# A deformable convolution and two gated recurrences on one core: forty column places for each parity, the table's writes on two queues, and the last tiles' norms and sums in another order

## The chip, the core and the metric

The kernel runs on one core of a Trainium2 chip. A core has TensorE (PE: matrix products and transposes into PSUM), VectorE (DVE), ScalarE (ACT), GpSimd (POOL) and SyncE (SP); DMA transfers are started by SP, POOL or ACT and carried by 16 DMA engines. The metric is the device time of one execution in microseconds (us), lower is better. All numbers are float32.

## The reference

`x` has 4 images of 256 channels on 64 x 64 positions. Two layers follow one another:

```python
x = x + _L0_conv_ref(_ln_c(x), ...)          # deformable 3x3 convolution of the channel-normalized x
t = _to_tokens(x)                            # (4, 4096, 256)
t = t + _L0_ffn_ref(_ln_t(t), ...)           # gated recurrence over the 4096 positions
x = _from_tokens(t, x)
x = x + _L1_conv_ref(_ln_c(x), ...)          # channel gate
t = _to_tokens(x)
t = t + _L1_ffn_ref(_ln_t(t), ...)
```

The deformable convolution computes 27 numbers per position by an ordinary 3x3 convolution (18 offsets, 9 masks), samples the normalized `x` bilinearly at the nine moved places, multiplies by the masks and applies a 256 x 256 matrix per tap. The recurrence has a projection `x U` and a recurrent product `h V` for each gate; a step is `c = h*c + i*g`, `h = o*tanh(c)`. The channel gate takes mean, maximum and standard deviation over the 4096 positions for each image and channel, subtracts the median of an image's 768 numbers, cubes, weighs and sums them, and multiplies the normalized `x` by a sigmoid of that.

## The kernel before

**Tiling.** A tile is a column of one parity: 128 partitions hold 4 images by 32 rows (even or odd), 256 channels lie along the free axis; 64 columns and two parities give 128 tiles. `RING` is 40 places of one tile each in SBUF (`ring`); a pool "square" has ten buffers of four tiles' size.

**Prepare** (`prepare`, 0 to about 266 us). The 64 columns go in 17 groups, most of four columns. Each group g is loaded from DRAM (`load`), both parities; VectorE takes the statistics (`stats`, `norm_of`; `together` says which groups share one), ScalarE normalizes in place (`norm`); `to_table` writes the normalized columns into a table in DRAM, eight writes a group (four images, two parities), each entry holding two neighbouring columns; PE turns a column (`turned`: four transposes) and multiplies it by the offset weights (`taps`: products into `zacc`); `summed` adds the pieces into `z`, `offsets` turns them into the 27 numbers a position (`om`), `samples` makes of these the places and weights of the sampling, and `keep` stores them in `plan`. The ring is split into two halves of 20 places (`M`), one for each parity, so a group can be loaded only when the table writes of an earlier group have left its place: in iteration g the kernel writes group g+1 and loads group g+4. The writes of both parities and of `plan` are started by SP, the loads from the fifth group on by POOL, in the order in which the loops issue them. `borders` writes zeros around the table (24 writes), on SP, ahead of all other table writes.

**Sampling** (`sample_and_recur`, about 270 to 2240 us). 576 slots; in slot s the kernel issues the gathers of two taps five slots ahead (POOL, indirect, into two "square" buffers), the scaling (ACT), the combination of the four corners (DVE), the transposes (PE, PSUM `tr`), the copy to SBUF (ACT) and 8 products into `acc`. The first gather needs the whole table.

**First recurrence.** Each of the 128 rows of a step is a stretch of 32 rows of an image; 144 steps go over the tiles in `ORDER`, the last 16 tiles first as a warm-up. Step n has its place at slot `step_slot(n)` = 52 + 4.5 n, so about the last 25 steps lie behind the sampling and run alone. A step: `recur` (`ga<-h`, `gb<-h`), `gates_of` (ACT: `tg`, `ti`, `to`, `th`), DVE's `cell` and `h`, and `project_part` for the next step (`ga<-cm`, `gb<-cm`). The gates `i` and `g` share the PSUM bank `ga` (pool of one buffer), `o` has `gb`.

**Fillers.** Everything else around the steps is given to a list (`Spare.give`) with its engine, earliest slot and cost, and `Spare.run` takes from it, in each slot and engine, what fits a budget (`BESIDE` beside the sampling, `ALONE` after it). The fillers: `added` turns `h` back, `add` adds it to the ring and sums the channels; `spread` squares (ACT); `norms` computes 1/std for eight tiles by three Newton steps (DVE, lists `first`, `second`, `last`); `styled` computes for the gate the normalized values and their squares (`y`, ACT, two tiles); `lanes` and `highest` add these up and take the maximum (DVE).

**Tail and gates** (2414 to 2474 us). For the last two pairs `summed` multiplies the sums (`lanes`, `y`) by `own`, a 128 x 4 matrix that adds the 32 partitions of an image, into `ys` (4 x 256); a copy and four transposes bring that to `pq`. `Gate.gates` computes mean, maximum and deviation (`u`), sends them through DRAM to all partitions, ranks them for the median, and computes the gate.

**Second recurrence** (`gated_lstm`, 2480 to 3266 us) and the output follow.

Of the kernel before, what the change touches and what calls it, by code (L numbers as in the profile page):

```python
# [19 lines left out]
P = 128  # L20
# [70 lines left out]
def prepare(tc, pools, const, wts_, x_in, table, errands):  # L91
# [7 lines left out]
    stp, gp, vp, ps_tr, ps_ac, ps_ms, ps_a, ps_b, sm, cm_p, yp = (  # L99
        pools[n] for n in ("chunk", "square", "v", "tr", "acc", "misc", "ga", "gb", "small", "cm", "y")  # L100
    )

    M = RING // 2
    cols = pools["ring"].rearrange("p (e m) c -> p e m c", e=2)
# [107 lines left out]
    def keep(o, w):  # L212
        for e in range(2):
            nc.sync.dma_start(plan[e * (W // OC) + o], w[:, e])
# [22 lines left out]
    def columns(g, lo, hi):  # L237
        return cols[:, :, at[g] + lo : at[g] + hi]

    def load(g, engine):  # L240
        if g < N:
            c, n = groups[g]
            for e in range(2):
                engine.dma_start(columns(g, 0, n)[:, e], x_in[:, e * W + c : e * W + c + n])


    together = [[0]] + [[g, g + 1] for g in range(1, N, 2)]
    sts, norms = {}, {}

    def stats(g):  # L250
        if g >= N:
            return
        gs = next(gs for gs in together if g in gs)
        if g == gs[0]:
            st = sm.tile([P, 20, 6], F32, name="st", tag="sth")
            sts[gs[-1]] = st, []
        st, of = sts[gs[-1]]
        for j in range(groups[g][1]):
            for e in range(2):
                nc.vector.bn_stats(st[:, len(of)], columns(g, j, j + 1)[:, e, 0])  # L260
                of.append((g, j, e))
        if g == gs[-1]:
            rs, low = norm_of(nc, sm, st[:, : len(of)], 1e-6, 20)
            for i, (h, j, e) in enumerate(of):
                norms.setdefault(h, []).append((columns(h, j, j + 1)[:, e, 0], rs, low, i))
# [6 lines left out]
    def to_table(g):  # L272

        c, n = groups[g]
        if c + n == W:
            nc.gpsimd.memset(columns(g, n, n + 1), 0.0)
        if g == 0:
            nc.gpsimd.tensor_copy(again, columns(0, 0, 1)[:, :, 0])
        elif at[g] == 1:
            last = groups[g - 1][1] + more[g - 1]  # L280
            nc.gpsimd.tensor_copy(columns(g, -1, 0), columns(g - 1, last - 1, last))
        if g == N - 1:
            nc.gpsimd.tensor_copy(columns(g, n, n + 1)[:, :, 0], again)
        lo, hi = int(g == 0), n + more[g]
        for e in range(2):
            for i in range(B):
                rows = tabs[i, :, 2 + e : 2 + H : 2].rearrange("x y c -> y x c")
                own = columns(g, lo - 1, hi)[i * R : (i + 1) * R, e]
                both = bass.AP(own.tensor, own.offset, [own.ap[0], [C, hi - lo], [1, 2 * C]])
                nc.sync.dma_start(rows[:, c + lo + 1 : c + hi + 1], both)  # L290
# [3 lines left out]
    def summed(g, zp):  # L294

        b0, b1 = blocks[g]
        z = gp.tile([P, 2, 6, BLOCK], F32, name="z", tag="square")
# [29 lines left out]
    nc.sync.dma_start(columns(0, 0, 2)[:, 0], x_in[:, split - 1 : split + 1])  # L327
    nc.scalar.dma_start(columns(0, 0, 2)[:, 1], x_in[:, W + split - 1 : W + split + 1])
    nc.sync.dma_start(woff, pools["w_off"])
    for g in range(1, 5):  # L330
        load(g, nc.sync)
    nc.sync.dma_start(gr, grid[0])
    nc.sync.dma_start(first, grid[1])
    borders()
# [3 lines left out]
    xt = turned(*(columns(0, 0, 1)[:, e, 0] for e in range(2)))  # L338
# [7 lines left out]
    for g, (c, n) in enumerate(groups):  # L346
# [4 lines left out]
        for j in range(n):  # L351
# [3 lines left out]
            if h < N:  # L355
                xt = turned(*(columns(h, i, i + 1)[:, e, 0] for e in range(2)))
            taps(banks[g], b0, b1 - b0, c + j, now, j == 0, j == n - 1)
            if j == 0 and g:
                summed(g - 1, banks.pop(g - 1))
# [4 lines left out]
        load(g + 4, nc.gpsimd)  # L364
        for o, w in sampled:
            keep(o, w)
        if g > 2 and errands:
            errands.pop(0)(nc)
        sampled = [(o, samples(o, om.pop(o))) for o in [*om] if g > 1 and blocks[g - 1][0] % OC]
        stats(g + 3)  # L370
# [164 lines left out]
class Spare:  # L535
# [6 lines left out]
    def give(self, engine, slot, us, do, room=lambda: True):  # L542
        self.todo.setdefault(engine, []).append((slot, us, do, room))

    def run(self, engine, slot, us, late=6):
        left = self.todo.get(engine, [])
        n = 0
        while n < len(left):
            ready, cost, do, room = left[n]
            if ready <= slot and room() and (cost <= us + 0.3 or slot - ready > late):  # L550
                del left[n]
                us -= cost
                do(slot)
            else:
# [6 lines left out]
def sample_and_recur(  # L561
# [15 lines left out]
    stp, gp, vp, ps_tr, ps_ac, ps_ms, ps_a, ps_b, sm, st, cm_p, yp = (  # L577
        pools[n] for n in ("chunk", "square", "v", "tr", "acc", "misc", "ga", "gb", "small", "state", "cm", "y")
    )
    ring = pools["ring"]  # L580
# [3 lines left out]
    PAIRS = NTILE * K // 2  # L584
    STEPS = len(ORDER)
    AHEAD = 5

# [14 lines left out]
    def gather(n):  # L602

        r = rounds[n] = {"units": [], "sq": [], "w": [], "v": []}
        for i in range(2):
# [5 lines left out]
            sq = gp.tile([P, 4 * C], F32, name="square", tag="square")  # L611
# [84 lines left out]
    def spread(n, k, b, j, slot):  # L696
# [9 lines left out]
        parts = (lo, hi - 2, hi) if b == STEPS // NB + 1 else (lo, hi)  # L706
# [19 lines left out]
    def norms(b, lo, hi, slot):  # L726
# [9 lines left out]
        )  # L736

# [5 lines left out]
        def first(slot):  # L743
# [5 lines left out]
            give("DVE", slot, 0.9, second)  # L749

        def second(slot):
            newton()
            newton()
            give("DVE", slot, 0.4, last)

        def last(slot):
# [6 lines left out]
            if hi > NB:  # L763
                first = max(lo - NB, 0)
                at = slice(ORDER[(b - 2) * NB] + first, ORDER[(b - 2) * NB] + hi - NB)
                nc.vector.tensor_copy(gate.rs[:, at], rs[:, NB + first - lo :])
                nc.vector.tensor_copy(gate.low[:, at], low[:, NB + first - lo :])
                for p in range(first // 2, (hi - NB) // 2):
                    give(
                        "ACT",  # L770
                        slot + 2 + (3 * p if b < STEPS // NB + 1 else 0),
# [5 lines left out]
        give("DVE", slot, 0.9, first)  # L777


    taken = {"xn": 0, "y": 0, "ms": 0, "ys": 0, "cm": 0}  # L780

    def room(tag, n):
        return lambda: taken[tag] < n
# [29 lines left out]
    def styled(b, p, slot):  # L813

        taken["y"] += 1
        n = b * NB + 2 * p
        y = yp.tile([P, 2, 2, C], F32, name="y", tag="y")

        def one(i):
            t = ORDER[n + i]  # L820
            for q, f in enumerate((AF.Identity, AF.Square)):
                normalize(nc, y[:, q, i], place(n + i)[:, 0], gate.rs, gate.low, t, f)

        def other(slot):
            one(1)
            through.update((n, n + 1))
            if n + 4 < STEPS:
                pending.append(y)
                give("DVE", slot + 1, 1.25, lambda s: lanes(y, s))
            else:  # L830
                give("PE", slot + 1, 1.88, lambda s: summed(y, n + 2 == STEPS, s))
                give("DVE", slot + 1, 0.75, lambda s: highest(y))

        one(0)
        give("ACT", slot, 1.15, other)

    def highest(y):
        nc.vector.tensor_max(gate.mx, gate.mx, y[:, 0])
        taken["y"] -= 1

    pending, order = [], []

    def lanes(y, slot):

        nc.vector.tensor_add(gate.lanes, gate.lanes, y)
        pending.pop()
        give("DVE", slot, 0.75, lambda s: highest(y))

    ys = []

    def summed(y, last, slot):

        order.append(last)
        assert not pending and order.index(True) == 1 if last else len(order) == 1
        for x in (gate.lanes, y) if not ys else (y,):
            if not ys:
                ys.append(ps_ms.tile([B, 2, C], F32, name="ys", tag="ys"))
            for i in range(2):
                for q in range(2):
                    nc.tensor.matmul(  # L860
                        ys[0][:, q],
                        gate.own,
                        x[:, q, i],
                        start=(x is gate.lanes and i + q == 0),
                        stop=(last and i + q == 2),
                        skip_group_check=True,
                    )
        if last:
            give("DVE", slot + 1, 0.6, lambda s: nc.vector.tensor_copy(gate.sum, ys[0]))
# [5 lines left out]
    START = 52  # L875
# [14 lines left out]
    def project_part(n, gs):  # L890
        cm = cms[n - n % 2][:, n % 2]
        if gs == SHARED[0]:
# [920 lines left out]
```

## Time and profile before

| what | before |
|---|---|
| runs shown | median 3270.24 us of 10 (3266.06 to 3275.22) |
| profiled execution | 3268.49 us |
| its span and mean granted clock | 3266.7 us, 0.971 |
| busy PE / PEld / DVE / ACT / POOL | 3040.8 / 2819.6 / 2589.9 / 2068.7 / 1580.5 us |
| busy share of PE, DVE, ACT | 93%, 79%, 63% |
| DMA | 829.53 MB, mean 254 GB/s |
| first gather issued on POOL | 269.55 us |
| last `ga<-h` of the first recurrence | 2414.00 us |

All times inside an execution are counted from the span's start. PE stands for matrix products and transposes, PEld for weight loads beside them, SPq for SP's own DMA instructions. A row "A <- B: us, times, longest" says how long an engine stood ahead of writing A because B was not ready. All instructions go through a recording helper, so most rows carry the helper's line (L412) and are told apart by the names of their tiles, out<-in.

### The profile page before, as it was taken

The page shows a single profiled execution, that of the slowest core. Times are in us where ns is not written, and L with a number is a line of the kernel's source. Part 1 is how long each engine was busy: PE and PEld are TensorE (multiplying, and loading weights), DVE is VectorE, ACT ScalarE, POOL GpSimd, SP SyncE. Part 2 cuts the span into 40 slices and gives each one's busy share as a digit, 9 for nine tenths or more (in the row PEclk, how much of TensorE's full clock was granted, in tenths as well). Part 3 has the DMA queues.
Part 4 walks back from the last instruction along what each step waited for, and adds up shares of the span by engine and source line. Part 5 has one row for each costly group of instructions (what it writes and reads, how often), then busy time and mean ns, then how long its engine had stood idle before and what let it go on. Part 6 is the DMA issues. An engine that isn't in the chain of part 4 may idle for free.

```text
span 3266.7 us, 61458 instructions
## 1 busy us (share of the span) xinstructions
PE 3040.8 (93%) x20370; PEld 2819.6 (86%) x20370; DVE 2589.9 (79%) x7218; ACT 2068.7 (63%) x5448; POOL 1580.5 (48%) x1495
## 2 busy tenths in 40 slices
PE   4767889999999999999999999998965999999998
PEld 4666779999999999999999999998854999999997
DVE  3446988888898999999999999995456777777774
ACT  3544566666676776776776776776655666666664
POOL 0005776776676776776677677671000022222221
PEclk8888999999999999999999999999986999999999
DMA  7879999989999999999989989993002244444442
GB/s 235 262 208 325 397 364 329 331 323 344 320 324 344 324 325 345 326 322 342 332 324 338 338 323 330 343 329 103 14 30 81 69 136 145 153 151 151 149 143 86
DMA packets 324278, 829.53 MB, mean 254 GB/s; under 512 B 104640, under 2 KB 112192, under 8 KB 319088
## 3 DMA queue, kind: packets, MB, share of 16 engines
q0 software_dynamic: 181856, 648.64, 55.0%
q1 hardware_dynamic: 141952, 176.61, 16.8%
q8 instruction: 164, 2.69, 0.3%
q14 instruction: 162, 1.33, 0.1%
q10 hardware_dynamic: 144, 0.26, 0.0%
HBM read 702.25 MB, written 123.12 MB: 253 GB/s over the span
## 4 chain that ended last, share of the span: by engine, by line
PE 80%; issue 8%; DMA 5%; DVE 4%; ACT 1%; SPq 1%; POOL 0%; ACTq 0%; POOLq 0%; DVEq 0%
PE acc L412 27%; PE ga L412 12%; PE gacc L412 7%; PE gtr L412 7%; PE tr L412 7%; PE gb L412 6%; DMA square<-table,used 4%; PE ggb L412 4%; PE gga L412 4%; PE zacc L412 2%; PE xt L412 1%; PE om L412 1%; DMA ring<-in_x_dram 1%; DVE st L412 1%; DVE v L412 1%
## 5 line engine op out<-in xcount | busy, mean ns | idle before, releaser
L412 POOL DMA_INDIRECT square<-table,used x1152 | 1380.5, 1198 | 624.2 <-DVE h L412 153.4
L412 DVE SCALAR_TENSOR_TENSOR v<-square,used,v 128x256 f32<-128x256 f32 x3456 | 1411.4, 477 | 56.0 <-ACT v L412 52.4
L412 PE MATMUL acc<-wconv,vt 128*128 128x256 f32 x4608 | 1098.3, 381 | 22.1 <-ACT vt L412 19.1
L412 PEld LDWEIGHTS acc<-wconv,vt 128*128 128x128 f32 x4608 | 832.9, 191 | 122.4 <-ACT vt L412 32.5
L412 ACT COPY vt<-tr 128x512 f32<-128x512 f32 x576 | 335.8, 583 | 520.4 <-PE tr L412 520.2
L412 ACT ACTIVATE v<-square,used 128x256 f32<-128x256 f32 x1152 | 534.9, 512 | 100.8 <-DMA square<-table,used 93.4
L412 PE MATMUL tr<-ident,v 128*128 128x128 f32 x2304 | 348.5, 274 | 17.0 <-DVE v L412 17.0
L412 DVE TENSOR_TENSOR tg<-tg,ti 128x256 f32<-128x256 f32 x284 | 120.2, 423 | 278.9 <-ACT ti L412 278.4
L412 PEld LDWEIGHTS tr<-ident,v 128*128 128x128 f32 x2304 | 273.9, 141 | 32.0 <-DVE v L412 13.3
L412 PEld LDWEIGHTS ga<-cm,Us 128*128 128x128 f32 x2272 | 273.9, 192 | 22.3 <-ACT ti L412 16.3
L412 PE MATMUL ga<-cm,Us 128*128 128x128 f32 x2272 | 279.3, 276 | 11.4 <-ACT ti L412 11.4
L412 PEld LDWEIGHTS ga<-h,Vs 128*128 128x128 f32 x2256 | 272.0, 192 | 5.9
L412 PE MATMUL ga<-h,Vs 128*128 128x128 f32 x2256 | 274.7, 275 | 0.0
L412 POOL DMA_DIRECT2D hd<-sqh x60 | 35.0, 583 | 409.5 <-DVE sqh L412 402.6
L412 POOL DMA_DIRECT2D ring<-hd x240 | 144.9, 632 | 165.3 <-DMA hd<-sqh 145.3
L412 ACT ACTIVATE tg<-gacc,bs 128x128 f32<-128x128 f32 x284 | 88.9, 364 | 185.0 <-PE gacc L412 185.0
L412 DVE TENSOR_TENSOR h<-to,th 128x256 f32<-128x256 f32 x282 | 119.0, 422 | 92.8 <-ACT th L412 92.7
L412 PEld LDWEIGHTS gacc<-h,Vs 128*128 128x128 f32 x1128 | 147.4, 192 | 15.1 <-DVE h L412 7.8
L412 PE MATMUL gacc<-h,Vs 128*128 128x128 f32 x1128 | 150.2, 276 | 6.3 <-DVE h L412 6.3
L412 PEld LDWEIGHTS gb<-cm,Us 128*128 128x128 f32 x1136 | 147.2, 192 | 6.0
L412 PEld LDWEIGHTS gb<-h,Vs 128*128 128x128 f32 x1128 | 146.0, 192 | 5.9
L412 PE MATMUL gtr<-h,Vs 128*128 128x128 f32 x1128 | 149.8, 276 | 0.0
(202 smaller groups left out, 4469.8 us busy)
## 6 DMA issues: line engine op xcount, KB each, us to landing
table<-ring SPq DMA_DIRECT2D x112, 256.0 KB
square<-table,used POOLq DMA_INDIRECT x1152, 6.6
ring<-x2d SPq DMA_DIRECT2D x18, 1024.0 KB
ring<-in_x_dram SPq DMA_DIRECT2D x65, 256.0 KB
x1d<-ring SPq DMA_DIRECT2D x64, 256.0 KB
x2d<-ring SPq DMA_DIRECT2D x16, 1024.0 KB
xd<-sqx SPq DMA_DIRECT2D x64, 256.0 KB
cm<-xd SPq DMA_DIRECT2D x256, 64.0 KB
```

Of the source, the lines that this page charges most:

```text
L412: ins = op(*args, **kw)
```

## The change

1. **Places.** Each parity gets 40 places: the even columns use all of `ring`, the odd ones a new constant tile `squares` of the same shape, which takes the room of the pool "square"; the gathers of sampling use slices of it, still ten in turn. Loads are issued as far ahead as the places allow (`old` names the latest group whose table writes a group's place has to wait for): the first ten groups at the start, partly on POOL, later ones when the writes of `old` lie two groups back.
2. **Queues.** Even table writes go on SP, odd ones on POOL; the writes of `plan` go on POOL; the borders are written after the iteration of the second group.
3. **Statistics** of group g+3 are issued in the middle of the iteration instead of at its end, with groups paired one later; `z` uses another pool.
4. **Steps alone.** Odd steps from the 119th on put `ga` and `gb` into the PSUM banks `acc` and `tr`, which sampling has left; `y` may use freed slices of `squares`; other budgets; in the last block the norms are computed in parts of four and of two tiles, at once and ahead of the list (`urgent`), and written straight into the gate's tiles where they can be.
5. **Sums.** `Gate.add` multiplies 128-column pieces of `lanes` and `y`, as the stationary operand, by `own` into `pq` directly; `ys`, its copy and the four transposes go. For the last two tiles (`ending`) VectorE computes the normalized values and ScalarE the squares, VectorE adds the two tiles.

The diff's core:

```diff
 def prepare(...):
-    M = RING // 2
-    cols = pools["ring"].rearrange("p (e m) c -> p e m c", e=2)
+    M = RING
+    cols = pools["ring"], pools["squares"]
...
     def keep(o, w):
         for e in range(2):
-            nc.sync.dma_start(plan[e * (W // OC) + o], w[:, e])
+            nc.gpsimd.dma_start(plan[e * (W // OC) + o], w[:, e])
...
+    old = []
+    for g, (c, n) in enumerate(groups):
+        own = range(at[g] - 1, at[g] + n + more[g])
+        old.append(max((h for h in range(g - 1) if at[h] + groups[h][1] + more[h] > own[0] and at[h] < own[-1] + 1), default=-1))
...
-    together = [[0]] + [[g, g + 1] for g in range(1, N, 2)]
+    together = [[0], [1]] + [[g, g + 1] for g in range(2, N - 1, 2)] + [[N - 1]]
...
     def to_table(g):
...
-        for e in range(2):
+        for e, engine in enumerate((nc.sync, nc.gpsimd)):
...
-                nc.sync.dma_start(rows[:, c + lo + 1 : c + hi + 1], both)
+                engine.dma_start(rows[:, c + lo + 1 : c + hi + 1], both)
...
-        z = gp.tile([P, 2, 6, BLOCK], F32, name="z", tag="square")
+        z = yp.tile([P, 2, 6, BLOCK], F32, name="z", tag="y")
...
-    for g in range(1, 5):
-        load(g, nc.sync)
+    there = 1
+    while old[there] < 0:
+        load(there, *((nc.sync, nc.sync) if there < 3 else (nc.gpsimd, nc.gpsimd)))
+        there += 1
     nc.sync.dma_start(gr, grid[0])
     nc.sync.dma_start(first, grid[1])
-    borders()
     stats(0)
...
-            if j == 0 and g:
-                summed(g - 1, banks.pop(g - 1))
+            if j == 0:
+                if g:
+                    summed(g - 1, banks.pop(g - 1))
+                stats(g + 3)
...
         if g + 1 < N:
             to_table(g + 1)
-        load(g + 4, nc.gpsimd)
+        while there < N and old[there] <= g - 2:
+            load(there, nc.gpsimd, nc.gpsimd)
+            there += 1
         for o, w in sampled:
             keep(o, w)
+        if g == 1:
+            borders()
...
         sampled = [(o, samples(o, om.pop(o))) for o in [*om] if g > 1 and blocks[g - 1][0] % OC]
-        stats(g + 3)
 class Spare:
     def run(self, engine, slot, us, late=6):
...
                 do(slot)
+                n = 0
 def sample_and_recur(...):
-            sq = gp.tile([P, 4 * C], F32, name="square", tag="square")
+            k = (2 * n + i) % SQUARES
+            sq = squares[:, 4 * k : 4 * k + 4].rearrange("p n c -> p (n c)")
...
-        parts = (lo, hi - 2, hi) if b == STEPS // NB + 1 else (lo, hi)
+        parts = range(lo, hi + 1, {STEPS // NB + 1: 2, STEPS // NB: 4}.get(b, hi - lo))
...
-            give("DVE", slot, 0.9, second)
+            if n0 >= LAST:
+                second(slot)
+            else:
+                give("DVE", slot, 0.9, second)
...
+                if n0 == STEPS - 2:
+                    ending(slot)
+                    return
...
+    def ending(slot):
+        n = STEPS - 2
+        (y, _), (both, _) = result(slot), result(slot)
+        for i in range(2):
+            t = slice(ORDER[n + i], ORDER[n + i] + 1)
+            x = place(n + i)[:, 0]
+            nc.vector.tensor_scalar(y[:, 0, i], x, gate.rs[:, t], gate.low[:, t], ALU.mult, ALU.add)
+            normalize(nc, y[:, 1, i], x, gate.rs, gate.low, t.start, AF.Square)
+        for q in range(2):
+            nc.vector.tensor_add(both[:, q, 0], y[:, q, 0], y[:, q, 1])
+            gate.add(nc, both, (0,), (q,))
+        highest(y, 0)
...
+        other = n % 2 and step_slot(n) > PAIRS + 8
         if gs == SHARED[0]:
-            ga = ps_a.tile([P, 2, NC, P], F32, name="ga", tag="ga")
+            at, tag = (ps_ac, "acc") if other else (ps_a, "ga")
+            ga = at.tile([P, 2, NC, P], F32, name="ga", tag=tag)
...
-            G[n][gs[0]] = ps_b.tile([P, NC, P], F32, name="gb", tag="gb")
+            at, tag = (ps_tr, "tr") if other else (ps_b, "gb")
+            G[n][gs[0]] = at.tile([P, NC, P], F32, name="gb", tag=tag)
...
-    ALONE = {"ACT": (0.3, -1, 1.6, 1.2, 0.3), "DVE": (0.5, -1, 1.3, 1.0, 0.5), "PE": (-1, 0.3, 0.3, 2.0, 0.3)}
+    ALONE = {"ACT": (0.3, -1, 2.9, 0.3, 0.3), "DVE": (0.5, -1, 3.2, 0.8, 0.5), "PE": (-1, 0.3, 0.3, 2.0, 0.3)}
+    END = {"ACT": (0.3, -1, 2.9, 0.3, 0.3), "DVE": (0.4, -1, 4.0, 0.4, 0.4), "PE": (-1, 0.3, 0.3, 2.0, 0.3)}
+    LASTLY = {"ACT": (0.3, -1, 1.0, 0.3, 0.3), "DVE": (0.4, -1, 0.0, 9.0, 9.0), "PE": (-1, 0.3, 9.0, 9.0, 9.0)}
 class Gate:
+    def add(self, nc, x, tiles, sums):
+        new = self.pq is None
+        if new:
+            self.pq = self.pools["misc"].tile([P, 2, NC, B], F32, name="pq", tag="ys")
+        for q in sums:
+            for k in range(NC):
+                for i in tiles:
+                    nc.tensor.matmul(
+                        self.pq[:, q, k],
+                        x[:, q, i, k * P : (k + 1) * P],
+                        self.own,
+                        start=(new and q + k + i == 0),
+                        stop=(len(tiles) == 1 and q + k == 2),
+                        skip_group_check=True,
+                    )
...
-        pq = ps_ms.tile([P, 2, NC, B], F32, name="pq", tag="ys")
-        for q in range(2):
-            for k in range(NC):
-                nc.tensor.transpose(pq[:, q, k], self.sum[:, q, k * P : (k + 1) * P], ident[:B, :B])
+        pq = self.pq
```

## The prediction, written before the changed kernel ran

> **What bounds the kernel now.** I read first the page's forty slices (81.7 us each), to see where the engine that is busy 93% of the span is not:
>
> ```profile
> PE   4767889999999999999999999998965999999998
> PEclk8888999999999999999999999999986999999999
> DMA  7879999989999999999989989993002244444442
> ```
>
> Three places have an idle PE: the first slices, slice 28, and 29 to 30. Between them lies sampling, where PE has 1789.78 of the 1790.00 us from 450 to 2240; only a change of PE's work could help there. The second recurrence (2480 to 3266) has PE busy 97%. The order of the instructions is the same in both kernels from the first sampling slot to the end of sampling and through the second recurrence, so I forecast no change in them and go to the three places.
>
> First the prepare stage, by the table of windows (busy us of PE, PEld, DVE, ACT, POOL; clock; DMA share; GB/s):
>
> ```profile
> 50.00:100.00 50.00, 20.02 (x93) 17.91 (x92) 20.47 (x77) 12.94 (x26) 5.39 (x10) 0.69 0.87 269
> 200.00:250.00 50.00, 32.11 (x162) 29.31 (x163) 20.10 (x78) 20.98 (x44) 3.30 (x6) 0.76 0.60 172
> 300.00:350.00 50.00, 44.96 (x225) 35.64 (x225) 46.65 (x121) 29.95 (x66) 38.18 (x38) 1.00 1.03 407
> ```
>
> No engine is full here, nor are the DMA engines, which reach 1.03 only when the gathers run. So a chain bounds it, and the waits of 0 to 265 us (us in total, times, longest) show its links:
>
> ```profile
> POOL ring L412 <- DMA table<-ring: 88.8, 11, 22.8
> ACT ring L412 <- DVE low L412: 68.8, 8, 15.2
> PEld zacc L412 <- ACT xc L412: 49.9, 8, 13.7
> DVE st L412 <- DMA ring<-in_x_dram: 32.9, 7, 10.0
> ```
>
> Read upwards: the load of a later group waits on POOL until the table writes that still read its place have landed; the statistics wait for the load, the normalization for the statistics, the turning and the taps for that. The order on SP's queue and the end of the stage come from two timelines:
>
> ```profile
> 11.45 22.44 SPq L412 DMA_DIRECT2D table<-zero  x24
> 33.99 11.50 SPq L412 DMA_DIRECT2D table<-ring  x16
> ```
>
> ```profile
> 56.26 0.54 POOL L412 DMA_DIRECT2D ring<-in_x_dram  x1 [22.80 <-DMA table<-ring]
> ...
> 269.55 1.36 POOL L412 DMA_INDIRECT square<-table,used  x1 [58.95 <-DVE fl L412]
> ```
>
> The first table write leaves 22 us late, behind 24 border writes; the first load that has to wait goes at 56.26; the first gather, which needs the whole table, at 269.55 (last table issue 263.4).
>
> Second, the steps of the first recurrence that run alone (PE's timeline):
>
> ```profile
> 2389.21 1.95 PE L412 MATMUL ga<-h,Vs 128*128 128x128 f32 x16
> 2390.99 1.06 PE L412 MATMUL gb<-h,Vs 128*128 128x128 f32 x8
> 2392.39 2.05 PE L412 MATMUL ga<-cm,Us 128*128 128x128 f32 x16 [0.34 <-ACT ti L412]
> 2394.28 1.06 PE L412 MATMUL gb<-cm,Us 128*128 128x128 f32 x8
> 2395.39 1.95 PE L412 MATMUL ga<-h,Vs 128*128 128x128 f32 x16
> ```
>
> A step takes 2395.39 - 2389.21 = 6.18 us, of which PE works 5.58 (the starts give 1.79, 0.89, 1.89, 0.89 and 0.22 for the transposes ahead of `h`, less 0.1 of refill). The rest is the wait for ScalarE to read the single bank `ga`.
>
> Third, the norms and sums from the last step to the gates (timeline):
>
> ```profile
> 2426.68 4.04 ACT L412 ACTIVATE y<-ring,glow,grs 128x256 f32<-128x256 f32 x8 [3.05 <-DVE glow L412]
> 2432.37 3.58 PE L412 MATMUL ys<-lanes,own 128*4 128x256 f32 x8 [12.59 <-DVE lanes L412]
> 2433.01 4.04 ACT L412 ACTIVATE y<-ring,glow,grs 128x256 f32<-128x256 f32 x8 [2.30 <-DVE gmx L412]
> 2435.74 4.60 PE L412 MATMUL ys<-y,own 128*4 128x256 f32 x16
> 2440.38 0.68 DVE L412 COPY lanes<-ys 4x512 f32<-4x512 f32 x1 [3.09 <-PE ys L412]
> ```
>
> The last `ga<-h` starts at T = 2414.00, and the spread that the gates need is written at 2445.2, T + 31.2.
>
> **Part 1, prepare: 40 places for each parity, writes on two queues, borders later.** Nothing is taken off the engines: same loads, statistics, taps and writes. What goes is the wait of loads for places: ten of the 17 groups are loaded at the start, and a later load follows the writes some six groups back, not four. The wait of 88.8 us ends there; what is late next? Three bounds. (1) PE: a column costs 2.08 us at full clock (transposes 0.43, taps 1.65), 64 columns 133, and the offsets of 17 groups 20 more, after a start of some 27: 180 to 190 us. (2) ScalarE: 6.9 us for a group of four columns, under PE's 8.3 plus 1.2. (3) The DMA engines: their share summed over 0 to 262 is 0.73, 0.87, 0.90 and 0.79 of 50 us and 0.66 of 62, 204 us for 60.84 MB, and the change moves the same bytes. So DMA is the next bound. Work starts at 8 us; at a share of 0.90, the best stretch while the table is written, the writes end at 8 + 204/0.90 = 235; at the gathers' 1.03 at 206. I take 0.97, between the two, because loads then always stand ready behind the writes: 218 instead of 262, a gain of 44 (27 to 56).
>
> The moves around it: the 24 borders go behind the second group's writes, so 22 us go from ahead of the first write, but their DMA time is in the 204. The early loads compete with the first group: 9.5 MB at 400 GB/s are 24 us, of which the first columns may lose some 5; the DMA bound does not feel it, the bytes are only earlier. POOL's queue now carries 68 table writes and 16 `plan` writes: a POOL load costs 0.53 us, a write by SP 0.97 in the median (302 to 2607 ns), so 84 issues are 45 to 80 us of POOL's 210, where it is busy 19. They can queue: a table write on POOL waits for ScalarE's normalization, and behind it stand the loads, but those are needed six groups on, some 60 us; I price it at nothing, the cover being these six groups (uncovered, up to 11.9 us as the row "POOL ring <- ACT ring" had it at most). On SP the write of `plan` goes away, half the table writes too: 131 us of issue become 66. The statistics of group g+3, moved ahead of the samples on VectorE, come about 5.5 us earlier; the samples behind them come 2.6 us later, and only the last samples are on the path, which have no statistics ahead of them: nothing. `z` in another buffer frees the first gathers from a VectorE wait, 0.3 us each: nothing beside DMA.
>
> The two queues themselves I price at nothing beyond the issue time, as SP was busy issuing only 153 of 262 us. The Trainium skill ("DMA: Bandwidth & Descriptors", section "Issuing engines are not separate DMA queues") says that transfers started by any engine end up on the same 16 DMA engines, so that a split saves only the sequencer's time. By this rule the 204 us stand as the floor; without it the rival B below is open. The shares of before can't tell, as loads on POOL and writes on SP already ran side by side there.
>
> **Part 2, second set of banks in the alone steps.** The odd steps from the 119th on use the idle `acc` and `tr` banks, so the projection no longer waits for `ti`. PE's 5.58 us become the bound unless the chain does: `h` is written 4.96 us after `ga<-h` starts (2414.00 to 2418.96), so 0.6 us are spare. The nearest row is the second recurrence, which has separate banks: 3240.24 to 3245.73, 5.49 a step. ScalarE's spare work must fit between `th` and the next `tg`, 3.0 us, and 2.06 (four y) + 0.9 (one spread) = 2.96 just does. I take 5.65: 23 steps lose 0.53 each, 12 us; a few irregular steps (2271.17 to 2279.63 took 8.46) may lose 1 more: 13. Bounds: 0, if ScalarE's list spills over every time, and 17, at 5.5 each.
>
> **Part 3, norms in pairs and sums by direct products.** From T: `h` at 5.0, the sum with the residual 6.1, the squares 7.5, twelve small VectorE operations of 0.2 run at once 9.9, y and its square 11.0 (two engines side by side), the additions and 128x4 products 12, the maximum 12.5, its turning and the spread's 16 small operations (2441.0 to 2445.2 = 4.2): T + 16.7 instead of 31.2. What goes: 24 products that spread 4 rows over 256 columns (2432.37 to 2440.34), the copy 0.68, the four transposes, and two waits of ScalarE (3.05 and 2.30). Gain 14, between 8 (the pair before last is late on ScalarE) and 17. The gates behind are the same, 2445 to 2474.
>
> **Sum.** 44 + 13 + 14 = 71 us off the profiled execution, 3268.49 (span 3266.7): 3197.5. The median of the runs is 3270.24, 1.8 higher; half of that added: 3198. A measurement here can tell 0.2%, 6.5 us, from no change.
>
> **Rivals.**
> - A, the DMA engines stay at the share that they had (0.90), since writes still come in bursts behind each group's normalization: 27 instead of 44, 3215. For it: ScalarE's 68.8 us behind VectorE are only partly due to loads. Against it: 0.90 was reached with loads held back.
> - B, two queues let the writes overlap more, so the 204 us shrink. The row of 222 to 240 (writes nearly alone, 243 GB/s at 90.6%) against 407 GB/s in the gathers speaks for it; then PE bounds, the end is at 190, a gain of 72: 3170.
> - C, the alone steps gain nothing, because ScalarE's lists fill the 0.04 us left and delay `tg`: 3198 + 13 = 3211.
> - D, the other side: POOL is in order, and its table writes hold its loads. In prepare, a period of 262/17 = 15.4 us a group would have to grow by 71/17 = 4.2, to 19.6. With 4 writes, 2 loads (1.06) and a `plan` write a group, that is so from 3.7 us a write on POOL. The longest write on SP took 2.6, a load on POOL 0.53; so it decides only if POOL needs far more for these short rows. At 4.5 us a write: 5 x 4.5 + 1.1 = 23.6 a group, 8.2 x 17 = 139 lost instead of 44 gained: 3270 + 139 - 27 = 3382.
> - E, the change does nothing: the loads come early, but the chain statistics, normalization, taps keeps its 15.4 us a group, and the tail's 27 us are mostly eaten by ScalarE: 3265.
>
> **Chances.** Forecast 0.51, A 0.17, B 0.13, C 0.08, D 0.08, E 0.03. The range takes in A, B and C and the low bounds of the three parts (27 + 0 + 8 = 35 gives 3234): 3168 to 3234. Faster by over 0.2% is all but D and E, 0.89; the same 0.03; slower 0.08.
>
> **What would show it.** First gather near 226 (213 to 243) instead of 269.55; POOL's wait for `table<-ring` gone or under 20 us; DMA share over 0.95 from 50 to 200; first table write near 20. Alone steps 5.6 to 5.7 apart and no `ga <- ti` wait. T + 16 to 18 for the spread. Wrong: a gap between table writes on POOL of over 4 us each, a longer sampling stage (1967 us from the first gather to 2237), or DVE's `st` still waiting for loads.

## The result and the profile after

The changed kernel takes 3196.55 us (median of 8 runs, 3191.61 to 3201.77) where the kernel before takes 3270.03 (28 runs): ratio 0.9776, 95% interval 0.9767 to 0.9785, 73.5 us less. The forecast was 3198. Four of the runs below (`again`, `one_queue`, `twenty`, `one_bank`) were taken at a time when every kernel took some 5% longer (the kernel before 3432 us, its sampling stage moving less per second: 309 GB/s from 450 to 2240 in `again` where the kernel before had moved 328), so they are read by their stages and by their ratio to the kernel before.

The first profiled execution took 3184.5 us, 12 below that median; a second one (`again_2` below) took 3195.68, with 3268.49 before, and is used for the account by stage:

| stretch | before | after (`again_2`) | difference |
|---|---|---|---|
| start to first gather | 269.55 | 213.87 | -55.7 |
| first gather to step 119 of the first recurrence | 1985.6 | 1980.4 | -5.1 |
| steps 119 to 121 | 16.1 | 19.6 | +3.6 |
| steps 121 to 143 | 142.8 | 139.5 | -3.4 |
| last `ga<-h` (T) to the spread `u` written | 31.2 | 19.0 | -12.2 |
| `u` to the start of the second recurrence | 37.2 | 38.0 | +0.8 |
| the rest | 784.3 | 783.5 | -0.8 |

Step 119 is the first that runs alone with the second set of banks. In the first profile the first five rows are 208.15, 1979.3, 16.9, 137.6 and 19.2. So two executions of the same program differ by some 6 us in the prepare stage, 3 in the first alone steps and 2 in the others; over all runs below that share the prepare stage, the first gather comes between 208 and 219. Of the 5.1 us in the second row, 3.9 lie ahead of the first product of sampling, which starts 13.5 us after the first gather instead of 17.4; nothing was forecast there.

Of the page of the first profile, the slices (79.6 us each) that answer to those of before:

```profile
PE   7968899999999999999999999998947999999998
PEclk9979999999999999999999999999978999999999
DMA  8999998899999998998999899891020344544442
```

The table of windows of the same kernel (columns as before):

```profile
50.00:100.00 50.00, 48.77 (x308) 45.18 (x307) 35.35 (x132) 36.78 (x76) 13.98 (x27) 1.00 0.90 240
200.00:250.00 50.00, 28.78 (x130) 22.73 (x131) 31.04 (x76) 18.62 (x38) 32.40 (x34) 0.73 0.99 368
```

PE has 48.77 us of work from 50 to 100, where it had 20.02 at a clock of 0.69; from 200 to 250 the gathers already run (DMA share 0.99, where it was 0.60). The waits of 0 to 240 us (us in total, times, longest):

```profile
POOL table L422 <- ACT squares L422: 32.8, 8, 9.0
...
POOL ring L422 <- DMA table<-ring: 27.2, 4, 15.4
...
ACT ring L422 <- DVE low L422: 19.5, 5, 10.2
```

The load's wait for table writes fell from 88.8 to 27.2 us (16.3 in `again_2`), the normalization's wait from 68.8 to 19.5; the wait of VectorE's `st` for loads is no longer among the large ones. New is the first row: the table writes on POOL wait for ScalarE. SP's and POOL's timelines:

```profile
20.00 22.13 SPq L422 DMA_DIRECT2D table<-ring  x12
42.22 17.88 SPq L422 DMA_DIRECT2D table<-zero  x10
```

```profile
208.15 1.08 POOL L422 DMA_INDIRECT squares<-table,used  x1 [21.68 <-DMA ring<-in_x_dram]
```

The first table write leaves at 20.0 instead of 34.0, the first gather at 208.15.

How long the DMA engines worked in the prepare stage is seen in one window each from the start to the last table write (columns as before), of `before`, `again_2`, `one_queue_2` and `twenty_b` (the last two are described below):

```profile
0.00:262.50 262.50, 173.29 (x930) 156.35 (x931) 118.86 (x457) 113.52 (x233) 18.80 (x39) 0.84 0.78 232
0.00:208.70 208.70, 160.97 (x960) 146.76 (x960) 124.36 (x501) 114.18 (x234) 64.79 (x125) 0.95 0.92 290
0.00:216.80 216.80, 163.67 (x960) 148.09 (x960) 123.91 (x500) 114.27 (x234) 19.18 (x43) 0.94 0.89 278
0.00:270.10 270.10, 170.40 (x916) 152.97 (x917) 115.85 (x467) 112.37 (x230) 65.21 (x127) 0.85 0.75 219
```

Share times length gives 205, 192, 193 and 203 us of DMA time.

A step that runs alone, on PE:

```profile
2278.33 1.95 PE L422 MATMUL ga<-h,Vs 128*128 128x128 f32 x16
2280.12 1.06 PE L422 MATMUL gb<-h,Vs 128*128 128x128 f32 x8
2281.01 1.95 PE L422 MATMUL ga<-cm,Us 128*128 128x128 f32 x16
2282.80 1.06 PE L422 MATMUL gb<-cm,Us 128*128 128x128 f32 x8
2283.69 0.38 PE L422 MATMUL ht<-ident,h 128*128 128x128 f32 x2
2283.91 1.95 PE L422 MATMUL ga<-h,Vs 128*128 128x128 f32 x16
```

5.58 us from one `ga<-h` to the next, and no bracket: PE does not wait in this step. Not all steps are like it: the 16 from step 121 to 137 take 96.3 us in this profile and 98.0 in `again_2`, 6.0 to 6.1 each, where they took 105.7. The end of the tail:

```profile
2354.22 1.09 ACT L422 ACTIVATE squares<-ring,glow,grs 128x256 f32<-128x256 f32 x2 [2.39 <-DVE glow L422]
2354.22 0.74 DVE L422 TENSOR_SCALAR squares<-ring,grs,glow 128x256 f32<-128x256 f32 x2
2354.99 0.78 DVE L422 TENSOR_TENSOR squares<-squares 128x256 f32<-128x256 f32 x2
2355.47 1.86 PE L422 MATMUL pq<-own,squares 128*128 128x4 f32 x8 [0.23 <-DVE squares L422]
```

Values on VectorE and squares on ScalarE start together, 12.3 us after the last `ga<-h` (T = 2341.91), and the products follow 1.25 us later; `u` is done at T + 19.2.

### The profile page after: what moved, and what is told of

It is laid out like the page before. It is cut to its first block, busy times and chain, and to the rows that moved or that the text cites. A ratio compares the mean times of both kernels' runs of the same rounds, so it can differ in the third digit from the quotient of the medians.

```text
span 3182.7 us, 61459 instructions
## 1 busy us (share of the span) xinstructions
PE 3021.8 (95%) x20382; PEld 2813.4 (88%) x20382; DVE 2592.8 (81%) x7264; ACT 2065.3 (65%) x5446; POOL 1609.4 (51%) x1583
## 4 chain that ended last, share of the span: by engine, by line
PE 81%; issue 8%; DMA 5%; DVE 4%; ACT 1%; SPq 1%; POOL 0%; ACTq 0%; POOLq 0%; DVEq 0%
PE acc L422 28%; PE ga L422 13%; PE gacc L422 8%; PE gtr L422 8%; PE tr L422 7%; PE gb L422 6%; PE ggb L422 4%; PE gga L422 4%; DMA squares<-table,used 3%; DVE v L422 1%; PE xt L422 1%; SPq L422 1%; PE zacc L422 1%; PE ht L422 1%; DMA table<-ring 1%
## 5 line engine op out<-in xcount | busy, mean ns | idle before, releaser
L422 POOL DMA_INDIRECT squares<-table,used x1152 | 1362.9, 1183 | 597.1 <-DVE h L422 148.2
L422 DVE SCALAR_TENSOR_TENSOR v<-squares,used,v 128x256 f32<-128x256 f32 x3456 | 1411.6, 477 | 66.5 <-ACT v L422 63.3
L422 PE MATMUL acc<-wconv,vt 128*128 128x256 f32 x4608 | 1099.6, 382 | 18.4 <-ACT vt L422 15.3
L422 ACT ACTIVATE v<-squares,used 128x256 f32<-128x256 f32 x1152 | 534.7, 513 | 109.6 <-DMA squares<-table,used 97.1
L422 ACT ACTIVATE tg<-gacc,bs 128x128 f32<-128x128 f32 x284 | 88.8, 363 | 184.6 <-PE gacc L422 184.6
```

The lines of the kernel that those rows point to most:

```text
L422: ins = op(*args, **kw)
```

## The experiments

The theory to test: in prepare, the 40 places (loads that need not wait) carry the gain and the DMA engines' time is the floor; in the steps, the second set of banks does; in the tail, the direct sums do. No run takes the tail's changes back, so what is said of the tail rests on the timelines.

**`again`** (no edit, taken with `one_queue`, `twenty` and `one_bank`) and **`again_2`** (no edit, taken with `one_queue_2`, `stats_late` and `best10`).

> The changed kernel unaltered, for a second profile. The first profiled execution (3184.5 us) was 12 us under the median of its runs (3196.55). If the executions differ in the prepare stage, the first gather of this one comes some 10 us later than 208 us; if they differ elsewhere (the steps alone, the tail), the first gather is again at 208 +- 3. The median stays at 3197 +- 4.

> The changed kernel unaltered, as a control beside the three others, whose first gathers and times are read against it. Expected: first gather 206 to 219, the last six steps 41.3 to 41.5 us, 3190 to 3200 where the kernel before takes 3270.

`again`: 3366 us, ratio to the kernel before 0.9824 (0.9786 to 0.9862); first gather 211.1, last six steps 41.5. `again_2`: 3195.68, ratio 0.9765 (0.9752 to 0.9778), first gather 213.9. In all five profiles with this prepare stage (`late_spread` 210.3 and `one_bank` 219.2 have it too) the first gather comes at 208 to 219.

**`twenty`**: the places halved.

```diff
-    M = RING
+    M = RING // 2
```

> Only 20 places of each parity are used, as before the change; queues, borders, statistics, banks and tail as changed. Theory (the loads' wait for places was the chain that bound the prepare stage): most of the 61 us come back, the first gather at 245 to 265, 3235 to 3255, and POOL's wait for table writes is 60 us or more again. Rival (the borders at the front and the late statistics were the cost): the first gather stays within 15 us of 208, under 3212.

First gather at 364 (269.55 before the change); 3517 us, ratio 1.025 (1.0216 to 1.0285). With 20 places the first load after the start comes behind the statistics of its own group in the program, so the statistics are taken of old columns and the load waits for them. This run says nothing about places alone; the next one keeps the loads where they were.

**`twenty_b`**: 20 places, loads issued where they were.

```diff
+    M = RING // 2
...
+    while there < 5:
...
+        while there < min(N, g + 5):
```

> 20 places of each parity and the loads issued as before the change (five groups at the start, group g+4 in iteration g); queues, borders, statistics, alone steps and tail as changed. The run called twenty issued the statistics of a group ahead of its load, so its 364 us say nothing on places alone. Theory (places carry the gain): first gather at 250 to 275. Second theory (rival D of the prediction, POOL's order: the table writes on POOL stand behind loads that wait): over 275, with POOL waiting over 100 us. Rival (queues, borders and statistics carry the gain): under 230.

First gather at 282.1, 12.6 us later than before the change and 68 later than in `again_2`; 3262.84 us, ratio 0.9982 (0.9973 to 0.9991), with the gain in sampling, steps and tail. So without the places the other changes in prepare bring no gain and seem to lose time. Waits of 0 to 262, and POOL's timeline:

```profile
DVE st L422 <- DMA ring<-in_x_dram: 99.3, 11, 19.7
POOL table L422 <- ACT squares L422: 94.0, 10, 14.8
```

```profile
83.50 0.56 POOL L422 DMA_DIRECT2D ring<-in_x_dram  x1 [28.16 <-DMA table<-ring]
...
122.55 2.26 POOL L422 DMA_DIRECT2D table<-squares  x4 [14.58 <-ACT squares L422]
124.80 0.56 POOL L422 DMA_DIRECT2D ring<-in_x_dram  x1
```

Two things show. The first load that waits goes at 83.50 (56.26 before), behind table writes that share SP with the borders from 42.5 to 75.2. And at 122.55 a load that could go stands behind four table writes that waited 14.58 us for ScalarE: the mechanism of rival D, though through waiting and not through long issues. Which of the two costs more was not separated.

**`places_only`**: all table and plan writes on SP, borders first, statistics at the end of the iteration.

```diff
-        for e, engine in enumerate((nc.sync, nc.gpsimd)):
+        for e, engine in enumerate((nc.sync, nc.sync)):
...
-            nc.gpsimd.dma_start(plan[e * (W // OC) + o], w[:, e])
+            nc.sync.dma_start(plan[e * (W // OC) + o], w[:, e])
...
+    borders()
     stats(0)
...
-                stats(g + 3)
...
+        stats(g + 3)
```

> Of the prepare stage's changes only the 40 places, the early loads and z's buffer are left: table and plan writes all on SP, borders at the front, statistics at the end of the iteration; alone steps and tail as changed. Theory (the places carry the gain, the queues and borders some 10 us): first gather at 222 to 235, against 269.55 before and 208 to 219 in the changed kernel. Rival (the queues and the borders carry it): first gather over 245.

First gather at 221.0, 48.5 us earlier than before the change; 3201.55 us, ratio 0.9795 (0.9781 to 0.9808). So the places bring 48.5 us, where the whole change brings 50 to 61 by the five profiles. With them stay the early loads, the pairing of the statistics and the other buffer of `z`, which were not taken apart.

**`one_queue`** and **`one_queue_2`**: the first two edits of `places_only` alone.

> All table writes and the plan writes go back to SP; everything else as changed. Theory (the DMA engines' time is the floor and the split of queues is worth only the time of issuing): SP's 136 + 24 + 16 issues of about 1 us are under 200 us, so the first gather moves by at most 5 us: 3197 to 3202. Rival (two queues let writes overlap, which is why the summed DMA share fell from 204 to 192 us): the first gather 12 to 30 us later, 3209 to 3227. Second rival (SP in order holds writes behind writes): the same sign, but with SP's wait rows full.

> All table and plan writes on SP, as in one_queue, which was run where the kernel before took 3432 us and the unaltered prepare stage ended anywhere from 211 to 219. Theory (two queues keep the DMA engines fuller: a share of 0.94 instead of 0.89 at the same 191 to 193 us of DMA time): first gather 8 to 15 us later than in the control, the time 8 to 15 us above it. Rival (the split is worth issue time alone): within 4 us.

First gathers 223.6 and 223.75, against 211.1 and 213.9 in the controls (219.2 in `one_bank`, taken with the first). The first run took 3381 us, ratio 0.986 (0.9828 to 0.9893; `again` 0.9824), the second 3201.04 against 3195.68 (ratios to the kernel before 0.9793, 0.9779 to 0.9806, and 0.9765, 0.9752 to 0.9778). So two queues are worth some 10 us of the first gather (4 to 13 by the pair chosen), of which 5 show in the time. The theory of the first run, at most 5, holds only with `one_bank` as the control. Three windows of `one_queue_2`:

```profile
50.00:100.00 50.00, 48.78 (x309) 45.21 (x308) 33.75 (x127) 36.34 (x75) 2.68 (x5) 1.00 0.78 243
100.00:150.00 50.00, 37.74 (x211) 34.29 (x210) 26.29 (x102) 25.90 (x55) 4.68 (x10) 0.86 0.96 307
150.00:200.00 50.00, 49.37 (x308) 45.55 (x307) 28.61 (x114) 30.36 (x64) 0.00 (x0) 1.00 0.90 249
```

The DMA share up to the last table issue is 0.89 of 216.8 us, in `again_2` 0.92 of 208.7: 193 and 192 us of DMA time. The second queue does not shorten the DMA time; the engines stand idle less. SP's DMA instructions last 179 us in sum of the 217 here; in `again_2` 116 of 209 on SP (157 of 203 in the first profile), and 61 on POOL beside them. But a single issue on SP lasts up to 6.5 us in `again_2`, and what the long ones wait for is not shown, so a well-filled SP is no proof that SP was the limit.

**`borders_first`**: the borders back to the front.

```diff
+    borders()
     stats(0)
...
-        if g == 1:
-            borders()
```

> The 24 border writes are ahead of all table writes again; everything else as changed. Theory (the DMA time is the floor, the borders only change places in it): the first table write some 20 us later, but the first gather within 5 us of the control. Rival (a late first write delays the whole chain of places): the first gather 12 to 20 us later.

First table write on SP at 49.4 instead of 20, and yet the first gather at 206.3 (`late_spread`, taken with it: 210.3); 3188.79 us, ratio 0.9748 (0.9734 to 0.9761). The theory held: the move of the borders brings nothing, perhaps loses some us.

**`stats_late`**: the statistics at the end of the iteration (the last two edits of `places_only`).

> The statistics of group g+3 are issued at the end of the iteration again, behind the samples; everything else as changed. Theory (they are three groups ahead, so their place is worth nothing): first gather within 3 us of the control. Rival (behind the samples they delay the normalization): POOL's and ScalarE's waits for low grow, first gather 5 to 12 us later.

First gather at 210.7, 3193.71 us against 3195.68, ratio 0.9763 (0.975 to 0.9777): no difference that can be told.

**`one_bank`**.

```diff
-        other = n % 2 and step_slot(n) > PAIRS + 8
+        other = False
```

> The alone steps use one set of banks again; budgets, norms and sums as changed. Theory (the single bank costs 0.6 us a step): steps of 6.18 instead of 5.58 from the 121st to the 137th, some 9 us, and less in the last six, which are late for another reason: 3197 + 9 to 12 = 3206 to 3209. Rival (the new budgets made the steps shorter): within 2 us of the changed kernel.

```profile
2492.50 2.05 PE L422 MATMUL ga<-cm,Us 128*128 128x128 f32 x16 [0.34 <-ACT ti L422]
```

The wait is back, the regular steps take 6.18 again; from step 121 to 137 it is 104.7 us, against 98.0 in `again` and 96.3 in `one_queue` and `twenty`, taken with it. The theory holds: 6.7 to 8.4 us for 16 steps. From 137 on it is 42.4 against 41.5: there the banks are not what binds. The time, 3390.51 us, ratio 0.988 (0.9845 to 0.9915), is 24 us over `again`; the two profiles differ by 40, 8 of them ahead of the first gather and 26 in sampling, which the edit does not touch, so the time says nothing of the banks.

**`late_spread`**: in the last eight steps the square behind `th`.

```diff
-            if n >= LAST:
+            if n >= STEPS - 1:
                 spread(n, 1, b + 2, NB + j, slot)
             else:
-                give("ACT", slot + 1, 0.9, lambda s: spread(n, 1, b + 2, NB + j, s))
+                give("ACT", slot + 1, 0.9, lambda s: spread(n, 1, b + 2, NB + j, s), urgent=n >= LAST)
```

> In the last eight steps ScalarE squares a row after th instead of ahead of the next tg (the last step excepted). Theory (ScalarE's square waits for VectorE's addition, which stands behind the norms, and tg stands behind the square): the last six steps take 35 to 37 us instead of 41.3, the spread u comes at T + 19 to 22, in sum 3 to 6 us faster than the changed kernel. Rival (VectorE's norms themselves are in tg's way): the last six still take 40 or more. The prepare stage is that of the changed kernel, so the first gather is a control: 208 to 219.

What binds the last steps of the changed kernel is seen in two timelines of `again_2`, of VectorE and of ScalarE:

```profile
2339.82 0.16 DVE L422 TENSOR_TENSOR glow<-nm,grs 128x2 f32<-128x2 f32 x1
2339.90 1.22 DVE L422 TENSOR_TENSOR lanes<-lanes,squares 128x1024 f32<-128x1024 f32 x1
2341.04 0.69 DVE L422 TENSOR_TENSOR gmx<-gmx,squares 128x512 f32<-128x512 f32 x1
2341.64 0.42 DVE L422 SCALAR_TENSOR_TENSOR ring<-ring,ht 128x256 f32<-128x256 f32 x1
```

```profile
2342.10 0.20 ACT L422 ACTIVATE nm<-su 128x1 f32<-128x1 f32 x1 [3.29 <-DVE ring L422]
2342.33 0.51 ACT L422 ACTIVATE sq<-ring,nm 128x256 f32<-128x256 f32 x1
2342.75 0.19 ACT L422 ACTIVATION_READ_ACCUMULATOR sq<-ring,nm 128x1 f32 x1
2342.84 0.60 ACT L422 ACTIVATE tg<-ga,bs 128x128 f32<-128x128 f32 x2
```

The norm's twelve operations, the sums and the maximum come ahead of the row's addition on VectorE; the row's square waits for that addition on ScalarE, and the step's `tg` stands behind the square. In `late_spread`, in the same place:

```profile
2325.51 0.42 ACT L422 ACTIVATE th<-cell 128x256 f32<-128x256 f32 x1 [0.43 <-DVE cell L422]
2325.83 0.19 ACT L422 ACTIVATE nm<-su 128x1 f32<-128x1 f32 x1
...
2328.99 0.62 ACT L422 ACTIVATE tg<-ga,bs 128x128 f32<-128x128 f32 x2 [0.38 <-PE ga L422]
```

The last six steps take 34.7 us instead of the 41.3 to 41.5 of all profiles with the steps of the changed kernel, and `u` comes at T + 20.0 instead of 19.0: 5.8 us gained between. The time is 3189.02, ratio 0.9752 (0.9739 to 0.9765); the changed kernel was not run beside it.

**`best10`**: `late_spread`, `borders_first`, and the budgets of the alone steps from slot 586.

```diff
-        elif s < PAIRS + 16 or s > step_slot(STEPS - 1) + 3:
+        elif s < PAIRS + 10 or s > step_slot(STEPS - 1) + 3:
```

> The borders ahead of the table writes, the square behind th in the last eight steps, and the budgets of the alone steps from slot 586 on instead of 592. Theory (ScalarE's list, taken without a budget until slot 592, holds up tg in the first alone steps, 10.5, 7.8, 8.2 and 8.1 us instead of 5.58): the steps from the 119th to the 143rd take 4 to 10 us less than in late_spread, and the time is 8 to 18 us under the control. Rival (that work has to be done anyway and shows up two steps later): steps as in late_spread, 3 to 8 us under the control.

3178.21 us (3176.02 to 3181.41), ratio 0.9716 (0.9703 to 0.9729) where `again_2` beside it has 0.9765: 17.5 us below the changed kernel, faster than both. Steps 119 to 121 take 14.2 us instead of 18.3 in `late_spread`, 121 to 137 94.6 instead of 97.9; the last six 35.2; first gather 206.4. Against the profile of `again_2` (18.4 us longer) the steps from 119 to 137 give 8.9 us, and the last six with the tail 5.3 (6.3 less 1.0); the prepare stage gives 7.5, uncertain by 6 as a single execution, and sampling takes 2.5 back. Not all of the 8.9 us can be put down to the budgets: `one_queue_2`, taken with it and with the old budgets, needs 111.8 us for the same steps, `again_2` 117.6 and `best10` 108.7, so the budgets are worth between 3 and 9.

## Why the prediction was right, and where its steps were not

The sum was 71 us and the account gives 72.8, but three terms were off and cancelled: prepare gave 12 us more than forecast, the alone steps some 10 to 13 less, and sampling, priced at nothing, gave 5. That 3198 came within 2 us of the median is luck; the mechanism was right for prepare and for the regular alone steps.

- **Prepare**: 44 forecast, 55.7 measured in `again_2`, at the edge of the term's bounds (27 to 56); the other profiles with the same stage have 50.4, 58.4, 59.2 and 61.4, three of them outside. The mechanism held: the load's wait for places was the chain (`places_only`, `twenty_b`), and with it gone the last table write goes at 203 to 209 us, with the DMA engines busy 0.92 to 0.94 of that and PE 161 to 163 us. That the DMA engines are what binds there is likely by their share but not isolated: POOL's table writes also wait 32.8 us for ScalarE. The size was off in three places of the step "8 + 204/0.97": the share is 0.92 to 0.94, not 0.97; the DMA time is 191 to 193 us, not 204; and the engines start before the 8 us (the first loads are issued at 1.2, before the change too). The DMA time fell with the places and not with the queues: 193 us with one queue in `one_queue_2` and 0.90 x 213.8 = 192 in `places_only`, but 203 with two queues and 20 places in `twenty_b`. In the packet records, the 18,019 packets of 2048 bytes up to the last table write take 116 ns each before the change, and the 18,018 of `one_queue_2` 108; why they are shorter is open.
- **Queues priced at nothing**: wrong by some 10 us of the first gather. The working compared SP's issues with the 262 us of before; SP's DMA instructions last 164 us of these 262.5, and with the load's wait gone and one queue 179 of 217, so far less slack is left. That this is what costs the 10 us is not shown. The Trainium skill ("DMA: Bandwidth & Descriptors", section "Issuing engines are not separate DMA queues") says that starting transfers from several engines saves only the sequencer's time, which it calls usually small beside the DMA itself; the trace agrees in that the DMA time was the same with one queue and with two (193 and 192 us).
- **Rival B** had the right sign, the 204 us did shrink, but to 192 and as much with one queue, so not by its cause; PE did not become the end at 190. **Rival A** had the share nearly right (0.92 to 0.94 with two queues, 0.89 and 0.90 with one), and missed that the DMA time would fall.
- **Borders, statistics, plan**: nothing forecast; for borders and statistics nothing found, and the writes of `plan` were moved only together with the table writes. The cover named for POOL, loads six groups ahead, was real: `twenty_b` shows the wait that comes without it.
- **Alone steps**: 13 forecast. From step 121 on 3.4 were measured; from 119 on, where the second banks begin, 158.9 us became 159.1 in `again_2` and 154.5 in the first profile, a gain of nothing to 4.4. The step "23 steps lose 0.53 each" holds for 16: 105.7 us became 98.0 (96.3 in the first profile), 7.7 to 9.4 saved, and undone by `one_bank`. Two things were missed. The first two alone steps grew from 16.1 to 19.6 us (15.5 to 19.7 in the profiles with the same steps); with the budgets from slot 586 they take 14.2. And the working of part 2 stopped at the 3.0 us of ScalarE behind `th` and did not place the squares that the changed kernel runs at once, ahead of `tg`: the last six steps grew from 37.2 to 41.5 us, and `late_spread` takes that back. Rival C's place (ScalarE in `tg`'s way) was right for these six.
- **Tail**: 14 forecast, 12.2 measured: T + 19.0 for T + 16.7. The working took `y` at T + 11; it came at T + 12.3, since the last step's `h` came later: its `tg` begins at T + 4.7 in the first profile, where before it was T + 2.0, again behind a square. ScalarE's lines of that step, before and after:

```profile
2415.99 0.63 ACT L412 ACTIVATE tg<-ga,bs 128x128 f32<-128x128 f32 x2 [1.96 <-PE ga L412]
...
2345.91 0.20 ACT L422 ACTIVATE nm<-su 128x1 f32<-128x1 f32 x1 [4.85 <-DVE ring L422]
2346.14 0.51 ACT L422 ACTIVATE sq<-ring,nm 128x256 f32<-128x256 f32 x1
2346.65 0.60 ACT L422 ACTIVATE tg<-ga,bs 128x128 f32<-128x128 f32 x2
```

- **Sampling and second recurrence** without change: the second recurrence moved by -0.8 us; sampling gave 5.1, 3.9 of them ahead of its first product. Why that product starts sooner after the first gather is open.
- **Its own signs**: the first table write near 20 came true (20.0), and PE's idle time ahead of `ga<-cm` that ended with `ti` fell from 11.4 to 0.4 us over the span. The first gather (213.87, in most other profiles 208 to 211, below the 213 named), the DMA share from 50 to 200 (0.93 in `again_2` and 0.96 in the first profile, for over 0.95), POOL's wait (16.3 and 27.2 us, for under 20) and the spread (T + 19.0, for 16 to 18) came true in part or not at all.

## What to carry to other kernels

When a buffer's place is the wait, look what else leans on that wait: here SP's issues had time to spare while it lasted, and the same reordering that ends the stage 12.6 us later with 20 places does not with 40. Work that is run at once "because it is urgent" stands in an in-order queue ahead of the step's own chain: put it behind the last operation that the chain needs. A total that comes out right does not show the terms right; an account by stage does.

## What was not expected of the hardware

An issue of a table write on SP lasts from 0.3 to 6.5 us within one stage of `again_2` (at most 2.6 in the kernel before), while POOL's issues of the other half of the same writes last 0.50 to 0.62. SP's 116 DMA instructions up to the last table write last 157 us in sum in one execution of the changed kernel and 116 us in another. And the DMA time of the same table writes and loads fell by 12 us when the loads no longer waited for places, with one queue as with two.
